# The first image's load in front of the weights, and side work between the first gathers, in a block-matching convolution kernel

## The chip, the cores and the metric

The kernel runs on one core of a Trainium2 chip. The metric is the device time of one execution in microseconds (us); smaller is better. A core has five engines with queues of their own: TensorE (PE, with its weight loads as PEld), VectorE (DVE), ScalarE (ACT), GpSimd (POOL) and SyncE (SP). SP, ACT and POOL issue DMAs in this kernel.

## The reference

Eight images of 32 channels and 128x128 pixels go through two layers. The first one normalises by groups of two channels, finds for each pixel the eight best of 25 shifts (of up to two pixels each way) by the squared difference over 3x3 patches, gathers the eight shifted copies, and runs a small convolutional network on the 256 channels. The second normalises again and applies one 5x5 kernel. Both add their input.

```python
def _patch_match_stack(x):                       # x: [8, 32, 128, 128]
    for dy in range(-2, 3):
        for dx in range(-2, 3):
            sh = x at (clip(y + dy), clip(x + dx))
            d = ((x - sh) ** 2).sum(1, keepdims=True)
            costs.append(_conv(d, ones_3x3, pad=1))
    _, idx = top_k(-costs, 8)
    return the 8 shifted copies of each channel  # [8, 256, 128, 128]

xb = _patch_match_stack(_gn(x))
dct = _conv(xb, dct_w, groups=C)
h = relu(_conv(_conv(xb, w1), w2, groups=CK, pad=1))      # w1, w3, w5: 256x256, 1x1
h = relu(_conv(_conv(h, w3), w4, groups=CK, pad=1))       # w2, w4, w6: depthwise 3x3
wiener = sigmoid(_conv(_conv(h, w5), w6, groups=CK, pad=1))
x = x + _conv(_conv(wiener * dct, inv_dct_w, groups=C), agg_w)
x = x + conv5x5(_gn(x), kernel)
```

## The kernel before

**Tiles.** An image lies in the tile xn: 128 partitions are 4 groups of rows times 32 channels, and each partition holds 38 rows (32 and a border of three) of 132 columns. load_image fills it with one large DMA for each row group (line 84, 32 partitions of 35 or 38 rows, 512 bytes a row) and six small ones that repeat the image's edge rows (line 89). The first image is loaded this way at the head of the program from ACT's queue, later ones from POOL's.

**Setup.** Behind the first image's DMAs in the text, SP loads the constants (cst), the depthwise weights (dwv, dwt) and the three 256x256 weights (nat_w1, nat_w3, nat_w5). POOL makes the block matrices dwd of the depthwise weights in 18 products (line 161); DVE reorders w1 (w_kc, line 178); TensorE transposes the three weights and ACT copies them to lw1, lw3 and lw5 (lines 188 and 189). The tiles of this setup have a pool of their own, with two PSUM buffers (ps_w).

**Matching.** For each image, prep takes statistics on DVE (st, line 348), normalises xn (line 359) and starts six rounds of squares: DVE subtracts shifted copies (df, line 413), ACT squares them (line 421), TensorE sums over channels (pd, line 428), ACT copies the sum to sm, and POOL stores it (sq). sources transposes the image to pixels first: TensorE (px), ACT (xs, line 384), POOL (DMAs xl, line 386, and xtd, line 394). costs loads the sums of one quarter of the rows of each row group into dsum (lines 461 and 468, 13 DMAs), sums them over 3x3 on DVE (v, line 477), transposes them (pt), copies them (ct, line 498) and picks the eight best with 32 pairs of maximum and index. places turns the indices to places (oc, then li, line 540) and stores them in DRAM (idxd).

**Gathering.** A unit is one step in gathering: gather_load fetches rows of pixels (xt) and the places, spread over the partitions (ib, line 574, from POOL); gather_select makes 0/1 selections from them on ACT (ib and sel, lines 588 and 589); gather_pixels multiplies them with the pixels on TensorE (pg, line 603) and ACT copies the result to xb (line 610). Buffers: five ib, four sel, three xt, four df, two ct.

**Order.** For PE, DVE and ACT the order of the program's text is kept (manual_schedule). All work that isn't the network itself is written as generators in four queues: D for work that costs DVE time, A for ACT, P and Q for TensorE. push puts a task in the queue that it names in a yield, with a cost and, as an optional third value, the number of turns before which it may not run. run("D", credit) takes tasks from D until their costs reach the credit; run of another letter takes all that are due. until repeats turns of D, A, P, Q until its condition holds. In the main loop, tick gives each step of the network its share of D. unit calls until by itself when gather_load needs places that aren't there yet. At the start prep(0) and mixes() (which makes ldct and lagg from dct_w, inv_w and agg_w) are pushed, and seven units are set off:

```python
for u in range(7):
    unit(gather_load, u)
    unit(gather_select, u - 2)
    unit(gather_pixels, u - 3)
```

Unit 0 needs the first quarter's places, unit 4 the second's. Everything behind this loop is the main loop, in which the three pointwise and depthwise convolutions of eight rows at a time, the gathers of the next rows and the side work of the next image are interleaved.

Of the kernel before, what the change touches and what calls it, by code (L numbers as in the profile page):

```python
# [8 lines left out]
F32 = mybir.dt.float32  # L9
# [6 lines left out]
P = 128  # L16
C, K, H, W = 32, 8, 128, 128
CK = C * K
NO = 25
R = 8  # L20
# [22 lines left out]
def bm3d_conv_preact(  # L43
# [16 lines left out]
    nc = tc.nc  # L60
# [9 lines left out]
    ps_x = ctx.enter_context(  # L70
        tc.tile_pool(name="ps_x", bufs=5, space=bass.MemoryType.PSUM)
    )
# [1 line left out]
        tc.tile_pool(name="ps_d", bufs=1, space=bass.MemoryType.PSUM)  # L74
    )

    def load_image(b, engine):

        xn = xnp.tile([P, HR, HX], F32, name=f"xn_{b}", tag="xn")
        for rg in range(4):  # L80
            s = slice(C * rg, C * (rg + 1))
            lo = 32 * rg - 3
            a, z = max(lo, 0), min(lo + HR, H)
            engine.dma_start(xn[s, a - lo : z - lo, 2 : 2 + W], x[b, :, a:z, :])
            for r in range(HR):
                y = lo + r
                if y < 0 or y >= H:
                    y = min(max(y, 0), H - 1)
                    engine.dma_start(
                        xn[s, r : r + 1, 2 : 2 + W], x[b, :, y : y + 1, :]  # L90
                    )
        return xn

    first = load_image(0, nc.scalar)
    cst = const.tile([P, C_N], F32, name="cst")
    nc.sync.dma_start(cst, consts)
    ident = cst[:, C_ID : C_ID + P]

    lw1 = const.tile([P, 2, CK], F32, name="lw1")
    lw3 = const.tile([P, 2, CK], F32, name="lw3")  # L100
    lw5 = const.tile([P, 2, CK], F32, name="lw5")
# [42 lines left out]
    nc.vector.tensor_scalar(inner, inner, -1.0, 1.0, op0=ALU.mult, op1=ALU.add)  # L144


    with tc.tile_pool(name="setup", bufs=1) as sp, tc.tile_pool(
        name="setup_ps", bufs=2, space=bass.MemoryType.PSUM
    ) as spp:
        dwt = sp.tile([P, 3, 4, 9], F32, name="dwt")  # L150
        for n, w in enumerate((w2, w4, w6)):
            for g in range(4):
                nc.sync.dma_start(
                    dwt[C * g : C * (g + 1), n],
                    w[:P].rearrange("(q c) o a b -> c q (o a b)", c=C),
                )
            nc.gpsimd.memset(dwd[0:C, n, 1], 0.0)
            for u in range(2):
                for dy in range(3):
                    s = slice(C * (u + dy), C * (u + dy + 1))  # L160
                    nc.gpsimd.tensor_tensor(
                        dwd[s, n, u],
                        cst[s, C_M32 : C_M32 + C]
                        .unsqueeze(1)
                        .unsqueeze(1)
                        .to_broadcast([C, 4, 3, C]),
                        dwt[s, n, :, 3 * dy : 3 * dy + 3].unsqueeze(3).to_broadcast([C, 4, 3, C]),
                        ALU.mult,
                    )
        wide = {}  # L170
        for name, w in (("w1", w1), ("w3", w3), ("w5", w5)):
            t = sp.tile([P, 2, CK], F32, name=f"nat_{name}", tag=f"nat_{name}")
            nc.sync.dma_start(t, w.rearrange("(m p) i a b -> p m (i a b)", p=P))
            if name == "w1":

                nat, t = t, sp.tile([P, 2, CK], F32, name="w1_kc")
                for m in range(2):
                    nc.vector.tensor_copy(
                        t[:, m].rearrange("p (k c) -> p k c", c=C),
                        nat[:, m].rearrange("p (c k) -> p k c", k=K),  # L180
                    )
            wide[name] = t
        for name, dst in (("w1", lw1), ("w3", lw3), ("w5", lw5)):
            for g in range(2):
                ps = spp.tile([P, CK], F32, name=f"ps_{name}_{g}", tag="ps")
                for m in range(2):
                    src = wide[name][:, m, g * P : (g + 1) * P]
                    nc.tensor.transpose(ps[:, m * P : (m + 1) * P], src, ident)
                nc.scalar.copy(dst[:, g], ps)

    xbp = ctx.enter_context(tc.tile_pool(name="xb", bufs=2))
    accp = ctx.enter_context(tc.tile_pool(name="acc", bufs=1))
# [21 lines left out]
    now = [0]  # L214

    def push(task):
        want = next(task, None)
        if want:
            which, cost, *wait = want
            queues[which].append((cost, task, now[0] + (wait[0] if wait else 0)))  # L220

    def run(which, credit=1e9):

        q, took = queues[which], 0.0
        for _ in range(len(q) if which != "D" else 1000):

            i = next(
                (
                    i
                    for i, (c, _, at) in enumerate(q)  # L230
                    if at <= now[0] and (c != PAIR or pairs[0] < 2)
                ),
                None,
            )
            if i is None or took >= credit:
                break
            cost, task, _ = q[i]
            del q[i]
            took += cost
            pairs[0] += cost == PAIR  # L240
            push(task)
        if which == "Q":
            pairs[0] = 0
        return took
# [8 lines left out]
    def group_stats(mv, name):  # L253
# [18 lines left out]
        yield from inverse_std(mr[:, 1:2], tmp[:, 0:1], tmp[:, 0:1])  # L272
        return mr

    def mixes():

        dq = work.tile([P, 2, K], F32, name="dq", tag="dq", bufs=1)
        src = dct_w.rearrange("(m h c i) k a b -> m h k c (i a b)", m=2, h=2, i=K)
        for k in range(K):
            for m in range(2):  # L280
                for h in range(2):
                    p = 64 * h + 8 * k
                    nc.sync.dma_start(dq[p : p + 8, m], src[m, (h + m + 1) % 2, k])
        m8 = work.tile([P, 8], F32, name="m8", tag="m16", bufs=1)
        yield "D", 1.0
        nc.vector.tensor_reduce(
            m8,
            cst[:, C_M32 : C_M32 + C].rearrange("p (a c) -> p c a", c=8),
            axis=mybir.AxisListType.X,
            op=ALU.add,  # L290
        )
        for m in range(2):
            nc.vector.tensor_tensor(
                ldct[:, m].rearrange("p (c i) -> p c i", i=K),
                m8.unsqueeze(2).to_broadcast([P, 8, K]),
                dq[:, m].unsqueeze(1).to_broadcast([P, 8, K]),
                ALU.mult,
            )

        iv = work.tile([P, 2, K], F32, name="iv", tag="iv", bufs=1)  # L300
        nc.sync.dma_start(iv, inv_w.rearrange("(m p) k a b -> p m (k a b)", p=P))
        ag = work.tile([C, CK], F32, name="ag", tag="xr")
        nc.sync.dma_start(ag, agg_w.rearrange("c i a b -> c (i a b)"))
        for m in range(2):
            yield "D", 0.5
            ib = work.tile([P, P], F32, name=f"ib_{m}", tag="xm")
            nc.vector.tensor_tensor(
                ib.rearrange("p (c k) -> p c k", k=K),
                cst[:, C_M16 : C_M16 + 16].unsqueeze(2).to_broadcast([P, 16, K]),
                iv[:, m].unsqueeze(1).to_broadcast([P, 16, K]),  # L310
                ALU.mult,
            )
            yield "P", 0
            ps = ps_x.tile([P, 512], F32, name=f"ps_ag_{m}", tag="x")[:, :C]
            nc.tensor.transpose(ps, ag[:, m * P : (m + 1) * P], ident[:C, :C])
            agt = work.tile([P, C], F32, name=f"agt_{m}", tag="agt")
            nc.scalar.copy(agt, ps)
            yield "P", 0
            ps2 = ps_x.tile([P, 512], F32, name=f"ps_ia_{m}", tag="x")[:, :C]
            nc.tensor.matmul(ps2, ib, agt, start=True, stop=True)  # L320
            nc.scalar.copy(lagg[:, m], ps2)
# [646 lines left out]
    def unit(stage, u, *rest):  # L968
        if 0 <= u < len(units) and units[u]:
            if stage is gather_load:  # L970
                at = (units[u][0], units[u][1] % 8 // 2)
                until(lambda: at in ready, 4.0)
            stage(*units[u], *rest)
# [13 lines left out]
    def tick(b, i):  # L987
# [3 lines left out]
        owed[0] -= run("D", owed[0]) if owed[0] > 0 else 0  # L991
        owed[0] = min(owed[0], 6.0)

    def until(cond, credit):
        while not cond():
            now[0] += 1
            run("D", credit)
            run("A")
            run("P")
            run("Q")  # L1000

    with tc.manual_schedule(engines=ORDERED):
        push(prep(0))
        push(mixes())
        xbd[0] = dram.tile([P, 2, H, W], F32, name="xbd_0", tag="xbd")
        for i in range(3):
            nc.gpsimd.memset(tb[i][0:64, :, 0], 0.0)
        for u in range(7):
            unit(gather_load, u)
            unit(gather_select, u - 2)  # L1010
            unit(gather_pixels, u - 3)
        u = 4
# [128 lines left out]
```

## Time and profile before

| what | value |
|---|---|
| median of 3 runs | 6841.84 us (6823.36 to 6853.25) |
| the profiled execution | 6843.88 us |
| its span, first to last instruction | 6842.1 us |
| mean granted TensorE clock | 0.976 |
| busy: PE, DVE, ACT, POOL | 93%, 86%, 74%, 47% of the span |
| DMA | 1021 MB, mean 149 GB/s |

The profile is of one execution. In its timeline a row has the start in us, the time from the first start to the last end of the merged instructions, engine and line, operation, tile written <- tile read, sizes and count, and in brackets how long the engine had stood and what ended that. A q behind an engine's name is its queue: there the row is the issuing of a DMA, not its transfer. A DMA that is named as the end of a wait is the one that came last by the profile, which can be another than the one waited for.

### The profile page before, as it was taken

Reading aid. Unit: us, or ns where it says so; the run is one execution under the profiler, and the core shown is the slowest. Engines: PE = TensorE matmul, PEld = TensorE weight load, DVE = VectorE, ACT = ScalarE, POOL = GpSimd, SP = SyncE. Lnnn points to the kernel's source line nnn. Section 1 sums busy time; section 2 is a strip of 40 time slices with the busy share of each in tenths; the row PEclk is TensorE's granted clock in tenths of the full one; section 3 lists DMA queues with packets and bytes.
Section 4 is the critical chain, followed back from the end, with each engine's and each line's share of the span. In section 5 each row is a group of like instructions: output and inputs, shape, how many; then the busy total and the mean of one; then the engine's idle time right before and its main releaser. Section 6 shows DMA issues by size and latency. Waiting matters only on the chain. (4 is left out here: it accounts for less than half of the span.)

```text
span 6842.1 us, 257025 instructions
## 1 busy us (share of the span) xinstructions
PE 6347.0 (93%) x113378; PEld 3356.7 (49%) x113378; DVE 5856.0 (86%) x8822; ACT 5064.5 (74%) x6698; POOL 3241.3 (47%) x5351
## 2 busy tenths in 40 slices
PE   4698999999999999999999999999999999999997
PEld 1354445455554445544554455555445455454553
DVE  6789988998889898898988898899888899877776
ACT  4687768777787777877778777877768777686772
POOL 6345436443464444644445444454435554344334
PEclk9899999999999999999999999999999999999998
DMA  3556656667566675665756667566665666566653
GB/s 80 135 148 151 155 138 162 154 161 155 144 158 160 148 167 137 162 148 154 163 134 158 164 147 168 136 165 158 151 148 148 159 160 149 138 168 156 155 151 77
DMA packets 809627, 1021.41 MB, mean 149 GB/s; under 512 B 255456, under 2 KB 619936, under 8 KB 808512
## 3 DMA queue, kind: packets, MB, share of 16 engines
q0 software_dynamic: 422432, 745.61, 43.8%
q1 hardware_dynamic: 381056, 256.86, 17.2%
q8 instruction: 892, 14.61, 0.9%
q10 hardware_dynamic: 5024, 2.49, 0.2%
q14 instruction: 223, 1.83, 0.1%
HBM read 553.25 MB, written 217.01 MB: 113 GB/s over the span
## 5 line engine op out<-in xcount | busy, mean ns | idle before, releaser
L695 DVE SCALAR_TENSOR_TENSOR acc<-tv,dwv,acc 128x1024 f32<-128x1024 f32 (+3 forms) x3264 | 4032.3, 1237 | 250.1 <-ACT acc L692 139.0
L721 PE MATMUL pw<-t,dwd 96*32 96x254 f32 (+7 forms) x31680 | 2143.5, 421 | 89.7 <-issue 41.9
L721 PEld LDWEIGHTS pw<-t,dwd 96*32 96x32 f32 (+1 forms) x31680 | 1107.0, 111 | 908.4 <-issue 437.1
L574 POOL DMA_DIRECT2D ib<-idxd x1024 | 570.8, 558 | 1780.0 <-ACT sel L589 1593.0
L588 ACT ACTIVATE ib<-ib,nplace 128x1024 bf16<-128x1024 bf16 x1024 | 1170.3, 1143 | 19.1 <-DMA ib<-idxd 19.1
L589 ACT ACTIVATE sel<-ib 128x1024 f32<-128x1024 bf16 x1024 | 1084.6, 1059 | 32.5
L665 PE MATMUL p<-acc,lw 128*32 128x256 f32 x16768 | 990.8, 382 | 23.8 <-ACT tv L649 22.7
L641 PE MATMUL pv<-acc,lw 128*128 128x512 f32 (+1 forms) x2112 | 973.5, 603 | 35.8 <-DVE acc L788 31.2
L761 POOL DMA_DIRECT2D xf<-xbd x1088 | 650.3, 631 | 321.2 <-PE pc L780 87.2
L665 PEld LDWEIGHTS p<-acc,lw 128*32 128x32 f32 x16768 | 556.2, 111 | 455.6 <-ACT tv L649 63.8
L649 ACT COPY tv<-pv 128x512 f32<-128x512 f32 (+2 forms) x784 | 437.9, 578 | 387.0 <-PE pv L641 378.3
L603 PEld LDWEIGHTS pg<-sel,xt 128*32 128x32 f32 x45056 | 576.2, 111 | 262.4 <-ACT sel L589 67.1
L421 ACT ACTIVATE df<-df 128x786 f32<-128x786 f32 (+2 forms) x576 | 467.9, 859 | 298.7 <-DVE df L413 295.9
L603 PE MATMUL pg<-sel,xt 128*32 128x48 f32 x45056 | 594.2, 207 | 90.4 <-ACT sel L589 47.5
L734 ACT ACTIVATE acc<-pw 128x512 f32<-128x512 f32 (+2 forms) x808 | 440.6, 573 | 256.4 <-PE pw L721 255.5
L413 DVE TENSOR_TENSOR df<-xn 128x786 f32<-128x786 f32 (+2 forms) x576 | 527.7, 967 | 118.7 <-PE pd L428 109.2
L641 PEld LDWEIGHTS pv<-acc,lw 128*128 128x128 f32 x2112 | 381.6, 191 | 477.6 <-issue 394.2
L699 ACT ACTIVATE acc<-acc 128x1024 f32<-128x1024 f32 (+3 forms) x408 | 417.0, 1022 | 229.7 <-DVE acc L695 229.5
L672 ACT COPY t<-p 128x512 f32<-128x512 f32 x800 | 424.6, 570 | 127.5 <-PE p L665 125.0
L692 ACT ACTIVATE acc<-tv,dwv 128x1024 f32<-128x1024 f32 (+3 forms) x408 | 454.6, 1114 | 50.6 <-PE pa L801 32.1
L641 PE MATMUL pv<-xb,lw 128*128 128x512 f32 x1024 | 476.2, 608 | 0.0
L665 PE MATMUL p<-xb,lw 128*32 128x256 f32 x8192 | 468.1, 380 | 3.5 <-DVE xy L906 3.5
(151 smaller groups left out, 5782.0 us busy)
## 6 DMA issues: line engine op xcount, KB each, us to landing
ib<-idxd POOLq DMA_DIRECT2D x1024, 256.0 KB, 4.5
xbd<-xb POOLq DMA_DIRECT2D x128, 1024.0 KB, 6.6
xf<-xbd POOLq DMA_DIRECT2D x960, 128.0 KB, 7.2
t<-t SPq DMA_DIRECT2D x792, 128.0 KB
t<-t SPq DMA_DIRECT2D x384, 256.0 KB
tv<-tv SPq DMA_DIRECT2D x384, 130.0 KB
xt<-xtd POOLq DMA_DIRECT2D x240, 176.0 KB, 4.6
xl<-xs POOLq DMA_DIRECT2D x256, 64.0 KB, 2.6
```

Of the source, the lines that this page charges most:

```text
L413: nc.vector.tensor_sub(df[:, :, ca:cz], xn[:, r0 : r0 + SR, ca:cz], xn[:, r0 + dy : r0 + dy + SR, ca + dx : cz + dx],)
L421: nc.scalar.activation(df[:, :, ca:cz], df[:, :, ca:cz], AF.Square)
L574: nc.gpsimd.dma_start(ib.rearrange("p k y x -> p (k y x)"), idxd[b][s4 // 8, s4 % 8, 4 * k0 : 4 * k0 + 8] .rearrange("k x -> (k x)") .part ...
L588: nc.scalar.activation(ib, ib, AF.Square, bias=nplace)
L589: nc.scalar.activation(sel, ib, AF.Relu, scale=-1.0, bias=1.0)
L603: nc.tensor.matmul(pg[C * j : C * (j + 1), :, xa:xz], xt[:, t], sels[j // 2][:, j % 2, :, xa:xz], start=True, stop=True,)
L641: nc.tensor.matmul(ps[:, :hr], lhsT[:, g, P:CK], src(g)[:, h : h + hr], start=g == 0, stop=g == 1,)
L665: nc.tensor.matmul(ps[C * r : C * (r + 1), e, :nb], lhsT[:, g, s], rows[:, r : r + 4 * nb - 3 : 4], start=g == 0, stop=g == 1,)
L692: nc.scalar.activation(acc, rows, AF.Copy, scale=tap)
L695: nc.vector.scalar_tensor_tensor(acc, rows, tap, acc, op0=ALU.mult, op1=ALU.add)
L721: nc.tensor.matmul(pt[u][C * j : C * (j + 1), ka:kz, :nb, xa:xz], dwd[0:hi, i - 1, u, j, dx + 1], t[0:hi, j, ka:kz, :nb, xa + dx : xz + dx ...
L761: nc.gpsimd.dma_start(xf[p : p + C, m, j0:j1], src[g, m, (h + m + 1) % 2, :, :, ya:yz])
```

## The change

Four edits. load_image takes several engines and gives them the row groups in turn: the first image is loaded from ACT (groups 0 and 2) and SP (groups 1 and 3), ahead of the constants and weights on SP. The setup of w1, w3 and w5 becomes a generator, weights, pushed between prep(0) and mixes(): its loads are issued there, its DVE work waits for at least eight turns, and the six pairs of transposes go one by one through the P queue; its tiles are parts of the main loop's acc tiles, and its PSUM comes from the common pool ps_x. The first DVE work of mixes may not run for ten turns. And in the loop over the first units, three turns of side work with a credit of 4.0 are run between the load of unit 2 and the selection of unit 0, and one between the load of unit 3 and the selection of unit 1.

```diff
-    def load_image(b, engine):
+    def load_image(b, *engines):
         xn = xnp.tile([P, HR, HX], F32, name=f"xn_{b}", tag="xn")
         for rg in range(4):
+            engine = engines[rg % len(engines)]
...
-    first = load_image(0, nc.scalar)
+    first = load_image(0, nc.scalar, nc.sync)
...
-        wide = {}
-        for name, w in (("w1", w1), ("w3", w3), ("w5", w5)):
-            t = sp.tile([P, 2, CK], F32, name=f"nat_{name}", tag=f"nat_{name}")
-            nc.sync.dma_start(t, w.rearrange("(m p) i a b -> p m (i a b)", p=P))
...
+    def weights():
+        natural, kc = {}, None
+        for i, (name, w) in enumerate((("w1", w1), ("w3", w3), ("w5", w5))):
+            t = accp.tile([P, 2, R * W // 2], F32, name=f"nat_{name}", tag=f"acc{i + 1}0")
+            natural[name] = t = t[:, :, :CK]
+            nc.sync.dma_start(t, w.rearrange("(m p) i a b -> p m (i a b)", p=P))
+        yield "D", 1.0, 8
+        nat = natural["w1"]
+        kc = accp.tile([P, 2, R * W // 2], F32, name="w1_kc", tag="acc31")
+        natural["w1"] = kc = kc[:, :, :CK]
+        for m in range(2):
+            nc.vector.tensor_copy(
+                kc[:, m].rearrange("p (k c) -> p k c", c=C),
+                nat[:, m].rearrange("p (c k) -> p k c", k=K),
+            )
+        for name, dst in (("w1", lw1), ("w3", lw3), ("w5", lw5)):
+            for g in range(2):
+                yield "P", 0
+                ps = ps_x.tile([P, 512], F32, name=f"ps_{name}_{g}", tag="x")
+                for m in range(2):
+                    nc.tensor.transpose(
+                        ps[:, m * P : (m + 1) * P],
+                        natural[name][:, m, g * P : (g + 1) * P],
+                        ident,
+                    )
+                nc.scalar.copy(dst[:, g], ps[:, :CK])
...
-        yield "D", 1.0
+        yield "D", 1.0, 10
...
+    def turn(credit):
+        now[0] += 1
+        run("D", credit)
+        run("A")
+        run("P")
+        run("Q")
+
     def until(cond, credit):
         while not cond():
-            now[0] += 1
-            run("D", credit)
-            run("A")
-            run("P")
-            run("Q")
+            turn(credit)
...
         push(prep(0))
+        push(weights())
         push(mixes())
...
         for u in range(7):
             unit(gather_load, u)
+            for _ in range({2: 3, 3: 1}.get(u, 0)):
+                turn(4.0)
             unit(gather_select, u - 2)
             unit(gather_pixels, u - 3)
```

In the two built programs the instructions of PE, DVE, ACT, POOL and SP differ in order only ahead of the second li copy; from there on they are the same, one by one. Ahead of it, w_kc comes behind the first 12 subtractions on DVE, the lw copies stand one by one between the squares of rounds 1 and 2 on ACT, dwd's 18 products stand directly ahead of the first xl DMA on POOL, the four xr_0 loads stand among the xl DMAs of POOL and the four xr_1 loads behind the first xt loads, and ACT runs unit 0's selections after six further squares of round 5, and unit 1's after the second ct copy.

More of the change, by code (lines that the diff above doesn't have):

```diff
@@ L144, in bm3d_conv_preact @@
     nc.vector.tensor_scalar(inner, inner, -1.0, 1.0, op0=ALU.mult, op1=ALU.add)
-    with tc.tile_pool(name="setup", bufs=1) as sp, tc.tile_pool(
-        name="setup_ps", bufs=2, space=bass.MemoryType.PSUM
-    ) as spp:
+    with tc.tile_pool(name="setup", bufs=1) as sp:
         dwt = sp.tile([P, 3, 4, 9], F32, name="dwt")
@@ L169, in bm3d_conv_preact @@
                     )
-        wide = {}
-        for name, w in (("w1", w1), ("w3", w3), ("w5", w5)):
-            t = sp.tile([P, 2, CK], F32, name=f"nat_{name}", tag=f"nat_{name}")
-            nc.sync.dma_start(t, w.rearrange("(m p) i a b -> p m (i a b)", p=P))
[L174 to L189, printed above, removed]
     xbp = ctx.enter_context(tc.tile_pool(name="xb", bufs=2))
```

## The prediction

> **What bounds the kernel now.** I read the page's forty slices first, then busy time by stretch, then the timeline of the start.
>
> ```profile
> span 6842.1 us, 257025 instructions
> ...
> PE   4698999999999999999999999999999999999997
> ...
> PEclk9899999999999999999999999999999999999998
> ```
>
> TensorE is full from the fifth slice on: only the first two slices, 342 us, have gaps that this change can touch.
>
> ```profile
> 0.00:20.00 20.00, 1.38 (x4) 0.69 (x4) 4.17 (x9) 0.00 (x0) 17.04 (x26) 1.00 0.64 118
> 20.00:40.00 20.00, 0.00 (x0) 0.00 (x0) 0.23 (x1) 0.94 (x1) 7.93 (x14) 1.00 0.41 66
> ...
> 140.00:160.00 20.00, 5.60 (x100) 3.06 (x100) 6.40 (x18) 11.25 (x13) 9.04 (x18) 0.56 0.46 136
> ...
> 300.00:320.00 20.00, 20.00 (x396) 11.16 (x392) 19.50 (x16) 17.70 (x24) 3.71 (x7) 1.00 0.51 124
> ...
> 2.00:4.00 2.00, 0.00 (x0) 0.00 (x0) 0.00 (x0) 0.00 (x0) 2.00 (x2) 1.00 0.94 249
> ...
> 22.00:24.00 2.00, 0.00 (x0) 0.00 (x0) 0.00 (x0) 0.00 (x0) 1.85 (x3) 1.00 1.18 226
> ...
> 32.00:34.00 2.00, 0.00 (x0) 0.00 (x0) 0.00 (x0) 0.00 (x0) 0.00 (x0) 1.00 0.95 215
> ```
>
> Columns are window, length, busy PE, weight load, DVE, ACT, POOL, then clock, DMA share, GB/s. For 40 us nothing computes, yet the DMA engines are half idle; when image data flows, it flows at 215 to 249 GB/s. From 300 us PE is full: what is saved ahead of that moves the end one for one.
>
> ```profile
> 0.74 0.43 ACTq L84 DMA_DIRECT2D xn<-in_x_dram  x1
> ...
> 8.14 16.09 POOL L161 TENSOR_TENSOR dwd<-cst,dwt 32x384 f32<-32x384 f32 x18 [1.66 <-DMA dwt<-in_L_conv_w_dram]
> ...
> 11.53 19.58 ACTq L84 DMA_DIRECT2D xn<-in_x_dram  x3
> ...
> 14.53 1.86 DVE L178 COPY w_kc<-nat_w 128x256 f32<-128x256 f32 x2 [7.80 <-DMA nat_w<-in_L_conv_w_dram]
> ...
> 37.29 1.74 ACTq L89 DMA_DIRECT2D xn<-in_x_dram  x3
> ...
> 41.02 4.84 DVE L348 BATCH_NORM_STATS2 st<-xn 128x6 f32<-128x512 f32 x8
> ...
> 45.90 0.37 DVE L352 BATCH_NORM_AGGREGATE mv<-st 128x2 f32<-128x48 f32 x1
> ...
> 50.14 2.89 DVE L359 TENSOR_SCALAR xn<-xn,mr_a 128x5016 f32<-128x5016 f32 x1
> ...
> 86.06 0.69 POOL L461 DMA_DIRECT2D dsum<-sq  x1
> ...
> 96.00 1.11 DVE L477 TENSOR_TENSOR v<-dsum 128x910 f32<-128x910 f32 x1 [4.89 <-DMA xl<-xs]
> ...
> 147.44 1.15 ACT L588 ACTIVATE ib<-ib,nplace 128x1024 bf16<-128x1024 bf16 x1 [9.40 <-DMA ib<-idxd]
> ...
> 156.43 0.50 ACT L498 COPY ct<-pt 128x400 f32<-128x400 f32 x1
> ...
> 182.19 0.48 ACT L540 CAST li<-pi 128x128 bf16<-128x128 f32 x2 [9.15 <-PE pi L538]
> ```
>
> The four large image loads are issued at 0.74, 11.53, 20.12 and 30.79, the last small one at 38.7. In the built program SP's and ACT's DMAs share eight semaphores in turn, and each waits for the DMA eight places before it; so the image waits on weight loads of SP, and they on it. Statistics start at 41.02, squares at 53.06. POOL issues DMAs without a gap over 0.2 us from 69.46 to 86.06, and DVE then waits 4.89 us for the dsum loads. At 138.03 ACT has written the first places and stands 9.40 us until they come back as ib; the squares' and costs' work behind it stands too.
>
> **What the Trainium skill says.** *DMA: Bandwidth & Descriptors*, "Issuing engines are not separate DMA queues": SP, ACT and GpSimd DMAs run on the same 16 engines and interleave, a second issuer saves issue time only. The trace agrees so far as 249 GB/s came from a single image load beside the constants; so I credit the second queue with no bandwidth, only with freed waits. *SBUF — State Buffer*, "Who interferes with whom": a GpSimd instruction that reads SBUF and a DVE instruction in a two-port mode, or with two SBUF inputs, take turns, the second fully blocked. The trace agrees for copies: at 14.53 two DVE copies took 0.97 us each amid POOL's dwd products, where a cast of the same 128x256 takes 0.28 (L520). For two-input subtractions beside dwd no run here shows it.
>
> **The change part by part.** T is when the image is in.
>
> 1. *Image.* Its ten DMAs now stand first; only SP's last two wait, for the first loads of either queue. 2.49 MB (queue q10) at 249 GB/s is 10.0 us; 0.74 issue, about 1.3 to first data (the window to 2.00 shows 12 GB/s), about 1.0 to land (data ended before 36, the next issue came at 37.29): **T = 13**. Bounds: 11.7 with no start-up to add; 24.3, if four loads cannot overlap and each takes the 5.9 us that 6.5 (30.79 to 37.29) less issue leaves.
> 2. *Statistics to squares.* Eight statistics 4.84, and some 0.5 for the five small constant operations now among them (an estimate; the last, L144, took 0.17); then 4.24 (45.90 to 50.14) and 2.89: squares at T + 12.6 = 25.6, without a lock.
> 3. *dwd.* The dwt loads now wait for the image's second ACT load (its semaphore). First products about 2 us after T, at 15 (iv, issued at 38.92, was used at 40.81). Alone 18 products end at 31.1, when the first xs copy is due (25.6 + 5.3), so they'd cost nothing. With the lock: four or five small DVE operations and the normalisation each meet a product of 0.83 half way, +1.9: squares at 27.5. By 24.6, 11 products are done, the normalisation blocks the next, 7 are left. They alternate with 7 subtractions of 0.90: 7 x 1.73 = 12.1, so dwd ends at 39.6 and the squares are 5.8 late.
> 4. *POOL to the first dsum load (86.06 now).* The third group of xl loads is issued when its xs copy is done, 13.4 behind the squares' start (66.49); from there POOL has no gap: five groups of xl (15.0), two of sq (4.5), and the four xr loads (2.5) that stood in idle time, 22.0. With the lock: 27.5 + 13.4 + 5.8 = 46.7 (POOL, free of dwd at 39.6 and of two groups at 45.6, isn't later), + 22.0 = 68.7: **17.4 gained**. Without: 25.6 + 13.4 + 22.0 = 61.0, **25.1**. ACT's moved copies (six lw at 0.4, four small ones) hide behind POOL: the seventh xs copy, 29.0 behind the squares now, comes at 27.5 + 29.0 + 5.8 + 1.4 = 63.7, and POOL turns to it at 65.7. DVE's moved pieces (about 2: two w_kc copies, ldct, ib) hide in its 4.89 wait, PE's transposes in its idle half; SP's 12 dwt, 3 nat and 32 dq loads, about 0.46 each unblocked, are issued by 35, the first needed after 38.
> 5. *From dsum to the places* nothing moves: the same order, DVE-bound (19.3 of 20 us).
> 6. *Turns.* The dsum sums of group 1 end at 141.8, transposes take 1.1: ct could be copied at 143.0 instead of 156.43, and the maxima start 13.4 earlier. ACT's eight ib and sel operations, 8.5 us, go between squares that leave it 1.7 idle each turn (1.67 to 1.69 in the timeline): the first four push the last squares and the second ct copy back, DVE waits some 2.8 for it against 1.3 now; the last four stand behind the second copy and run beside the maxima. POOL's new order puts the last dsum loads behind an ib load that waits for a selection; I put them out at about 170 on the old scale, when the indices are due. **11.9 gained** at the second li (182.19). Bounds 9.4, the stand alone, and 13.4.
> 7. *After that* every engine's instructions follow in the old order, and the gain is carried along; waits there are between them. The clock while PE starts is 0.50 to 0.64 and may change by little either way.
>
> Sum: 17.4 + 11.9 = 29.3. The profiled execution took 6843.88 (span 6842.1, 1.8 around it), 2.0 above the median 6841.84; 29.3 less is 6814.6 for such an execution, 6812.5 from the median.
>
> **Rivals.**
> - *A, as summed, lock and all:* 6812, own range 6800 to 6824. For it: the 0.97 us copies, the skill's sentence.
> - *B, no turn-taking between dwd and subtractions:* 25.1 + 11.9 = 37.0: 6805. For it: the trace has no such pair. Against: the copies.
> - *C, it doesn't do what it says: the loads stay serial behind one another.* T = 24.3, 11.3 worse than A: 18.0, 6824. For it: no two large image loads are ever in flight together in the trace. Against: at 13 to 18 us one shared the engines with the nat loads at 217 to 229 GB/s.
> - *D, slower: the granted clock.* From 300 us PE is the bound, some 6,500 us; each 0.01 of the mean clock (0.976 now) is worth 6,500 x 0.01 / 0.976 = 67 us. If 0.005 or more is lost, the gain is gone; with 0.0095 lost, 64 - 29 = 35 slower: 6876. For: the clock follows what ran before, and the start shows all from 0.50 to 1.00. Against: by 300 us it is at 1.00, and the work from there on is the same.
>
> **How the numbers follow.** 0.5%, about what a measurement of this kernel can tell from no change (its three runs span 0.44%), is 34 us. A has 0.55, B 0.33, C 0.05, D 0.07. A falls beyond 34 in four of ten (the working is good to some 5, a median to some 10), B in seven to eight of ten: faster 0.47. D gives slower over 0.5% in most cases: 0.06. The rest, 0.47, is within. The forecast is A's, 6812; the range, 6788 to 6832, takes in B with an early image, and C.
>
> **What would show it.** Right: statistics from 13 to 14, not 41; dwd products and first squares alternating, both near 1.7 us a pair; the first dsum load near 69; ACT with no wait over 3 us ahead of its first ib; second li near 153; then the old pattern, 29 earlier. dwd back to back and squares at 0.9 would mean B; image loads 6 us apart, C; a mean clock under 0.97, D. Wrong altogether: a new wait after the second li that gives the gain back.

## The result and the profile after

Over twelve executions each, the changed kernel takes 6803.94 us (median; 6798.84 to 6814.12) against 6833.18 for the kernel before: a ratio of 0.9959, 95% interval [0.9951, 0.9967], which is 28 us less (23 to 33). The profiled execution took 6809.07.

The page of the changed kernel, its span and two rows of its forty slices:

```profile
span 6807.3 us, 257036 instructions
...
PE   5798899999999999999999999999999999999997
...
PEclk8899999999999999999999999999999999999998
```

Only the first two slices have visibly more TensorE work than before. The clock row is not higher, and the mean granted clock of this execution is 0.973 against 0.976: the gain lies in the start, not in the clock. Busy time by stretch (window, length, busy PE, weight load, DVE, ACT, POOL, then clock, DMA share, GB/s):

```profile
2.00:4.00 2.00, 0.00 (x0) 0.00 (x0) 0.00 (x0) 0.00 (x0) 2.00 (x2) 1.00 0.98 210
...
12.00:14.00 2.00, 0.00 (x0) 0.00 (x0) 0.00 (x0) 0.00 (x0) 0.00 (x0) 1.00 1.28 180
...
16.00:18.00 2.00, 0.00 (x0) 0.00 (x0) 1.58 (x7) 1.27 (x1) 0.00 (x0) 1.00 0.24 20
```

The image flows without a break from 2 to 16 us at 180 to 210 GB/s, with the DMA engines' mean busy share above 1 from 4 us on (the times of several packets on one engine overlap). The 249 GB/s that the prediction counted on is not reached; what that number was stands below, under step 1. The timeline, queue by queue:

```profile
0.74 0.43 ACTq L85 DMA_DIRECT2D xn<-in_x_dram  x1
...
0.74 1.21 SPq L85 DMA_DIRECT2D xn<-in_x_dram  x2
...
23.42 22.99 SPq L291 DMA_DIRECT2D dq<-in_L_conv_dct_w_dram  x32
...
16.42 1.29 DVE L356 BATCH_NORM_STATS2 st<-xn 128x6 f32<-128x512 f32 x2 [15.49 <-DMA xn<-in_x_dram]
...
23.40 0.70 DVE L243 SCALAR_TENSOR_TENSOR tmp_a<-tmp_a,mv 128x1 f32<-128x1 f32 x1
...
26.77 3.31 DVE L367 TENSOR_SCALAR xn<-xn,mr_a 128x5016 f32<-128x5016 f32 x1
30.11 15.11 DVE L421 TENSOR_TENSOR df<-xn 128x792 f32<-128x792 f32 x12
...
18.10 21.87 POOL L160 TENSOR_TENSOR dwd<-cst,dwt 32x384 f32<-32x384 f32 x18 [10.14 <-DMA dwt<-in_L_conv_w_dram]
...
46.87 2.98 POOL L394 DMA_DIRECT2D xl<-xs  x4 [0.56 <-ACT xs L392]
...
68.67 0.69 POOL L469 DMA_DIRECT2D dsum<-sq  x1
...
120.48 0.41 ACT L548 CAST li<-pi 128x128 bf16<-128x128 f32 x2
...
125.84 0.49 ACT L506 COPY ct<-pt 128x400 f32<-128x400 f32 x1 [4.95 <-PE pt L502]
...
134.10 1.13 ACT L596 ACTIVATE ib<-ib,nplace 128x1024 bf16<-128x1024 bf16 x1
...
141.34 0.47 ACT L506 COPY ct<-pt 128x400 f32<-128x400 f32 x1
...
152.14 0.48 ACT L548 CAST li<-pi 128x128 bf16<-128x128 f32 x2 [3.87 <-PE pi L546]
...
163.91 0.56 POOL L567 DMA_DIRECT2D xt<-xtd  x1 [8.79 <-PE pg L611]
...
171.56 1.15 ACT L596 ACTIVATE ib<-ib,nplace 128x1024 bf16<-128x1024 bf16 x1 [9.47 <-DMA ib<-idxd]
```

Statistics start at 16.42 instead of 41.02, the first dsum load is issued at 68.67 instead of 86.06, and the second li cast starts at 152.14 instead of 182.19. ACT goes into its first ib at 134.10 without a wait for it; the squares and the ct copy of the next quarter now stand ahead of it. The wait of nearly 9.5 us that stands at 171.56 is an old one: the kernel before has it too, as 9.72 at 201.87.

### The profile page after: what moved, and what is told of

Same layout as the page of the kernel before. It is cut to its first block, busy times and chain, and to the rows that moved or that the text cites. A ratio compares the mean times of both kernels' runs of the same rounds, so it can differ in the third digit from the quotient of the medians.

```text
span 6807.3 us, 257036 instructions
## 1 busy us (share of the span) xinstructions
PE 6354.3 (93%) x113378; PEld 3352.8 (49%) x113378; DVE 5860.4 (86%) x8822; ACT 5064.6 (74%) x6698; POOL 3246.7 (48%) x5351
## 4 chain that ended last, share of the span: by engine, by line
PE 55%; DVE 23%; ACT 8%; DMA 6%; issue 5%; POOL 3%; SPq 0%; ACTq 0%; DVEq 0%; POOLq 0%
PE pw L729 18%; DVE acc L703 15%; PE pv L649 13%; PE p L673 12%; PE pg L611 4%; DVE df L421 3%; PE pc L788 2%; DMA t<-t 2%; PE p L902 2%; ACT df L429 2%; ACT ib L596 2%; DVE idx L514 1%; PE pa L809 1%; DMA xf<-xbd 1%; DVE acc L796 1%
```

## The experiments

Each ratio is to executions of the kernel before that were measured together with the run. From the ratio and their median I give microseconds: 0.001 is 6.8 us. Where a run is compared within its start, it is by the same instruction's start in the profile. Such starts scatter too, by up to 1.6 us: the first li of turns_only, ahead of which nothing was changed, starts 1.55 earlier than in the kernel before. Ends of single executions scatter by 10 us and more. "Lead" is how much earlier an instruction starts than in the profile of the kernel before, where the first four li casts start at 137.62, 182.19, 230.76 and 266.46.

**1. The two parts apart: the turns alone (turns_only), and all but the turns (no_turns).** The first is the kernel before with turn() and the loop; the second is the changed kernel without it:

```diff
-            for _ in range({2: 3, 3: 1}.get(u, 0)):
-                turn(4.0)
```

> The kernel before with the four turns of side work alone; image and weights load as before. Theory (the parts add up): statistics still start near 41, the first li stays at 138, ACT no longer stands for its first ib, the second li comes near 170 instead of 182.2, and all behind it follows: 12 us faster, ratio 0.998. Rival (the turns pay only behind the earlier image, or the saved wait comes back as another one behind the second li): second li near 170, but under 4 us at the end, ratio above 0.9994.

> The changed kernel without the four turns. Theory: the first dsum load stays at 68.7 and the first li at 120.5, ACT stands some 9.4 us for its first ib again, second li near 164.5: 17 to 18 us faster than before, ratio 0.9974. Rival (the turns carry the gain, the earlier image is lost in a wait for POOL): under 10 us, ratio above 0.9985.

Measured: turns_only 0.9992 [0.9984, 1.0], 5.5 us less; no_turns 0.9982 [0.9972, 0.9992], 12.3 less. The timeline of turns_only, then of no_turns, first and second li:

```profile
136.07 0.41 ACT L540 CAST li<-pi 128x128 bf16<-128x128 f32 x2
...
167.73 0.48 ACT L540 CAST li<-pi 128x128 bf16<-128x128 f32 x2 [3.87 <-PE pi L538]
```

```profile
120.71 0.41 ACT L548 CAST li<-pi 128x128 bf16<-128x128 f32 x2
...
130.53 1.15 ACT L596 ACTIVATE ib<-ib,nplace 128x1024 bf16<-128x1024 bf16 x1 [9.41 <-DMA ib<-idxd]
...
165.34 0.48 ACT L548 CAST li<-pi 128x128 bf16<-128x128 f32 x2 [9.20 <-PE pi L546]
```

What the turns remove is a wait of DVE for the ct copy behind ACT's first selections, here in the kernel before; in the changed kernel the same maximum starts at 126.36, right behind DVE's last subtraction.

```profile
156.96 0.20 DVE L505 MAX8 mx<-ct 128x8 f32<-128x25 f32 x1 [13.43 <-ACT ct L498]
```

From first to second li it is 31.66 us with the turns in either kernel (167.73 - 136.07; 152.14 - 120.48) and 44.63 and 44.57 without them: the turns are worth 12.9 to 13.0 us wherever the start stands. The rest of the change is worth the 16.9 by which the first li of no_turns leads. Together that is 29.8, against the changed kernel's 30.1. At the fourth li turns_only leads by 13.8 and no_turns by 16.4, together 30.2. At the end the two gains, 5.5 and 12.3, are smaller than the leads and than what was expected (0.998 and 0.9974). For the turns alone the whole interval, 0 to 11 us, lies below the lead of 13.8, so part of it was lost later on; where, these runs don't show. For no_turns the lead lies within the interval, 5 to 19 us.

**2. One queue for the image (one_queue).**

```diff
-    first = load_image(0, nc.scalar, nc.sync)
+    first = load_image(0, nc.sync)
```

> The changed kernel with the whole first image on SP's queue, still in front of all weights. Theory (being in front is what counts, the 16 DMA engines set the rate): image in at 15 to 18 us against 16.3, the first dsum load within 2 us of 68.7, the end within 2 us of the changed kernel, ratio 0.9955 to 0.9962. Rival (a queue alone makes no more than a large load in 6 us): image in at 24, everything 7 to 8 us later, ratio 0.997. Other rival (two queues disturb each other: 180 to 210 GB/s instead of 249): image in at 13, 3 us earlier, ratio 0.9955.

Measured: 0.9968 [0.9958, 0.9979]. Busy time while the image flows, then the timeline, DVE and ACT:

```profile
1.80:16.20 14.40, 0.00 (x0) 0.00 (x0) 0.00 (x0) 0.00 (x0) 6.16 (x13) 1.00 1.22 182
```

```profile
16.84 2.47 DVE L356 BATCH_NORM_STATS2 st<-xn 128x6 f32<-128x512 f32 x4 [15.91 <-DMA xn<-in_x_dram]
...
152.36 0.48 ACT L548 CAST li<-pi 128x128 bf16<-128x128 f32 x2 [4.12 <-PE pi L546]
```

Statistics start at 16.84, between the two profiles of the changed kernel (16.42, and 16.91 in after_again of experiment 5), and so does the second li (152.14, 152.36, 152.59). One queue keeps the transfers in flight just as well once nothing stands in front of them, so no gain of the second queue can be told from the scatter: what *DMA: Bandwidth & Descriptors* says in "Issuing engines are not separate DMA queues" holds here. Both rivals fall, the image at 24 and the image at 13. The ratio missed its range, 0.9955 to 0.9962, but its interval takes in the changed kernel's 0.9959.

**3. The load alone (load_only).** The kernel before with the image's load split over both queues, and the weights' work where it was:

```diff
-    first = load_image(0, nc.scalar)
+    first = load_image(0, nc.scalar, nc.sync)
```

> The kernel before with one part of the change alone: the first image goes over ACT's and SP's queues in turn; all weights, their transposes and the order of every engine's work stay as before. Theory (the place of the weights' side work on VectorE makes the front, not the load): the first statistics stand on VectorE behind the products that wait for SP's 32 dq loads; those are now issued behind two of the four image groups, as in the changed kernel, where they ended at 46.4 us against 38.9 in the kernel before. So the first statistics start at 48 to 49 us, not 40.2, the second li near 190 instead of 182.2, and the kernel is slower than before by about 8 us, ratio 1.001. Rival (the image's arrival is what was late): statistics at 16 to 25 us, a gain of 17 us as in the run without the turns, ratio 0.9975.

Measured: 1.0014 [1.0006, 1.0022], 9.6 us **slower**. (The kernel before starts its statistics at 41.02; the 40.2 of the expectation is the turns' run.) The timeline, SP's queue and DVE:

```profile
23.68 23.00 SPq L284 DMA_DIRECT2D dq<-in_L_conv_dct_w_dram  x32
...
46.64 0.23 DVE L294 TENSOR_TENSOR ldct<-m,dq 128x64 f32<-128x64 f32 x1 [20.26 <-DMA dq<-in_L_conv_dct_w_dram]
...
48.69 4.83 DVE L349 BATCH_NORM_STATS2 st<-xn 128x6 f32<-128x512 f32 x8
```

The image's last large load is issued at 3.12 on ACT's queue, as in the changed kernel, and the transfers run at 177 to 201 GB/s until 16 us; yet the statistics start 7.7 later than in the kernel before: on DVE, whose order is that of the text, they stand behind ldct and ib, products that need dq and iv, and SP is through with dq at 46.7. The lead at the first and second li is -7.6 and -7.5. So the early load is worth less than nothing here without moving the weights' side work behind the statistics.

**4. The lock: six products (six_products) and memsets in their place (memsets).** In the first, the second and third dwd groups are filled with zeros instead, so two thirds of the depthwise weights are left out:

```diff
+            if n:
+                nc.gpsimd.memset(dwd[:, n], 0.0)
+                continue
```

> The changed kernel with POOL's products for the first depthwise layer only: the twelve of the other two layers are left out and their blocks set to zero in POOL's idle time at the start. Lock theory: the six are done near 23.5, the normalisation takes 2.9 instead of 3.3, the first squares run at 0.9 us each instead of 1.5, the first dsum load comes near 64.5 instead of 68.7, and the end 4 us earlier than the changed kernel's, ratio 0.9953. Rival (POOL is late only because of its own DMAs, the lock costs nothing at the end): first squares at 0.9, but the first dsum load within 1 us of 68.7 and ratio 0.9959.

In the second, each product is replaced by two memsets:

```diff
-                    nc.gpsimd.tensor_tensor(
-                        dwd[s, n, u],
...
+                    for _ in range(2):
+                        nc.gpsimd.memset(dwt[s, n], 0.0)
```

> The changed kernel with its 18 GpSimd products for dwd replaced by 36 GpSimd memsets of 384 columns (two for each product) with the same waits; dwd is zero, so this part of the computation is left out. GpSimd is as busy beside VectorE's squares, but reads nothing. Theory (what alternates is the use of the port by any GpSimd instruction, as VectorE stood still in the kernel before while GpSimd wrote zeros at 4.5 us): squares that run beside memsets still take about 1.5 us each instead of 0.9, and end as late as GpSimd's work lasts. Rival (only GpSimd instructions that read lock VectorE out): every square takes 0.90 us as it does with six products, the normalisation 2.89, and the first dsum load is issued at 63.8 us or by GpSimd's own lateness, without long squares.

Measured: 0.9961 [0.9949, 0.9973] and 0.9956 [0.9942, 0.997]. First twelve subtractions and first dsum load of six_products; then POOL, the subtractions and the first dsum load of memsets:

```profile
29.21 10.77 DVE L424 TENSOR_TENSOR df<-xn 128x792 f32<-128x792 f32 x12
...
63.82 0.69 POOL L472 DMA_DIRECT2D dsum<-sq  x1
```

```profile
18.84 19.19 POOL L161 MEMSET dwt<- 32x384 f32 x36 [9.92 <-DMA dwt<-in_L_conv_w_dram]
...
29.80 7.23 DVE L414 TENSOR_TENSOR df<-xn 128x792 f32<-128x792 f32 x8
...
65.88 0.69 POOL L462 DMA_DIRECT2D dsum<-sq  x1
```

With POOL's products gone from that stretch, twelve subtractions take 10.77 us instead of 15.11 and the first dsum load comes 4.85 earlier. At the end nothing of this can be told: 0.9953 was expected of six_products, and its 0.9961 is nearer to the rival's 0.9959, with an interval that holds both. Beside memsets, which keep POOL busy until 38.0, the subtractions take 0.90 each (7.23 / 8), as if POOL stood still; that the first dsum load comes at 65.88 and not near 63.8 is POOL's own lateness, whose xl loads can start only at 37.97. My theory of this run fell: it is not any work of POOL's that locks out a two-input subtraction. What sets the products apart is that they read, as *SBUF — State Buffer* has it in "Who interferes with whom": with an instruction that reads, not with one that only writes. (A POOL instruction that reads one input only was not run.) The same page says that DVE in a two-port mode contends with GpSimd without that exception and that the one issued second is blocked. The longest of the products in the changed kernel and of the memsets here agree, if the normalisation runs in such a mode, which the trace doesn't name (minimum, median and maximum in ns):

```profile
L160 POOL TENSOR_TENSOR dwd<-cst,dwt x18: 827/832/3273, 18.1 to 38.5; 32x384 f32<-32x384 f32 x18
```

```profile
L161 POOL MEMSET dwt<- x36: 407/411/2927, 18.8 to 37.6; 32x384 f32 x36
```

One product and one memset are as long as the normalisation, 3.31 and 2.92 us, that they met. So a POOL that only writes is not always free beside VectorE. In the kernel before, a copy of 128x4 that takes 0.15 in the changed kernel took 2.04 beside POOL's memsets at the start, until the last of them ended at 6.5; that they held it up was not tested apart.

```profile
4.47 2.04 DVE L132 COPY neg<-cst 128x4 f32<-128x4 f32 x1 [3.54 <-DMA cst<-in_consts_dram]
```

**5. A version without the lock (later_products).** Nothing is left out: six products stay in place, twelve are issued once the main loop has begun, behind a copy on DVE (dwt in the constants' pool):

```diff
+    late = const.tile([P, C], F32, name="late")
...
+    products(0)
...
+                if s == 0:
+                    nc.vector.tensor_copy(late, cst[:, C_M32 : C_M32 + C])
+                    products(1)
+                    products(2)
```

> The changed kernel with only the six products of the first dwd group in place; the other twelve are issued on GpSimd once the main loop has begun, behind a copy on VectorE. Nothing is left out. Theory (twelve products beside the squares cost 5 us of the front, as the run with six products showed, and nothing waits for them until the first depthwise step): first dsum load at 63.8 us against 68.7, second li at 147.2 against 152.1; the order of GpSimd's loads around the third select step differs, so ACT's wait of 9.5 us for ib near 171 us may shrink too. End earlier than the changed kernel by 5 us, up to 14 if that wait goes: ratio to before 0.9955 to 0.9965 on this chip. Rival (the products lock out squares or selections later just as long, or a main-loop load waits behind them on GpSimd): no gain over the changed kernel in the same call, or a loss of up to 10 us.

> The changed kernel itself, on the same chip as the others of this call. If the second queue for the image is worth nothing, it stands where the run with one queue stood, within 3 us; if the lock's 5 us reach the end, the later products end 5 us ahead of it.

Measured side by side: later_products 0.9936 [0.9921, 0.9952], after_again (the changed kernel once more) 0.9961 [0.9949, 0.9974]; medians 6797.25 and 6816.16. The gain over the changed kernel is 17 us by the ratios, more than I expected, though the intervals overlap a little. (after_again stands 5 us below one_queue's ratio, not within 3; their intervals overlap widely.) The timeline of later_products:

```profile
64.05 0.69 POOL L476 DMA_DIRECT2D dsum<-sq  x1
...
147.50 0.48 ACT L555 CAST li<-pi 128x128 bf16<-128x128 f32 x2 [4.12 <-PE pi L553]
...
150.53 4.55 POOL L165 TENSOR_TENSOR dwd<-late,dwt 32x384 f32<-32x384 f32 x3
155.03 2.77 POOL L589 DMA_DIRECT2D ib<-idxd  x5
...
158.90 1.15 ACT L603 ACTIVATE ib<-ib,nplace 128x1024 bf16<-128x1024 bf16 x1 [1.44 <-DMA ib<-idxd]
...
187.77 0.48 ACT L555 CAST li<-pi 128x128 bf16<-128x128 f32 x2 [16.39 <-PE pi L553]
```

The second li leads by 34.7 (the lock's share, 4.6 over the changed kernel), the third by 43.0 against 30.3: another 8.1, as the wait for ib is 1.44 where it was 9.47. POOL's queue has another order here, with the xt_4 load behind the five ib loads; experiment 6 tests whether that is the reason.

**6. That wait by itself (xt_sync), and both (later_xt_sync).** In the changed kernel the xt_4 load waits on POOL's queue for TensorE until 163.91, and five ib loads stand behind it. In both runs SP issues it:

```diff
-                nc.gpsimd.dma_start(
+                (nc.sync if (b, s4) == (0, 4) else nc.gpsimd).dma_start(
```

> The changed kernel with one transfer moved to another queue: the xt_4 load, which waits on GpSimd's queue from 154.5 to 163.9 us for TensorE and has the ib loads of the second select step behind it, is issued by SyncE. Nothing is left out. Theory (this wait is what is late next once the first image is in early and the turns are taken): the five ib loads are issued at about 155.5 us instead of 165.35, ACT's wait of 9.5 us for ib at 171.56 us goes down to under 2, the third li cast comes near 191 instead of 200.4, and the end is 7 to 10 us earlier than the changed kernel's, ratio to before about 0.9948. Rival (ib's buffers, or TensorE's pixels, hold ACT up just as long): the wait keeps most of its 9.5 us or moves behind it, third li after 198, ratio 0.996.

> The kernel with the later products and the xt_4 load on SyncE's queue. In the run with the later products the wait for ib was 1.4 us already, so theory: no more than 1.5 us over that run, ratio to before 0.993 to 0.9945, third li at 186 to 188 us. Rival (the two gains add, 5 us of the lock and 9 of the wait on top of what the later products brought): third li near 180, ratio 0.992.

Measured: 0.9949 [0.9932, 0.9965] and 0.9943 [0.9929, 0.9957]. The timeline of xt_sync, SP's queue, POOL and ACT:

```profile
163.82 0.35 SPq L567 DMA_DIRECT2D xt<-xtd  x1
...
156.69 1.67 POOL L582 DMA_DIRECT2D ib<-idxd  x3 [0.52 <-DMA idxd<-li]
...
162.50 1.15 ACT L596 ACTIVATE ib<-ib,nplace 128x1024 bf16<-128x1024 bf16 x1 [0.22 <-DMA ib<-idxd]
...
191.39 0.48 ACT L548 CAST li<-pi 128x128 bf16<-128x128 f32 x2 [16.41 <-PE pi L546]
```

xt_4 is loaded no earlier, 163.82; but the ib loads no longer wait behind it, ACT's wait goes from 9.47 to 0.22, and the third li from 200.44 to 191.39: 9.1 us. With both, the third li comes at 188.67, near the 187.77 of the later products alone, so the wait that they had shortened is the one that this removes; the gains don't add. All three versions beat the kernel before, and their ratios lie 7 to 17 us below the two of the changed kernel (0.9959, 0.9961). Their intervals touch or overlap its; that they are faster than it rests on the leads of the start, and at the end is not shown for each. Which of the three is best these runs don't tell.

## Why the prediction was right, and where its sum was wrong

- **Case A came true**, 28 us against 29.3: products and subtractions alternate, the load's groups are in flight together (C would have had statistics at 24), the first dsum load at 68.67 for 68.7, the second li at 152.14 for 153. The median lies 8 below the forecast of 6812 because the kernel before has one of 6833.18 here, not 6841.84. Three of the signs missed: statistics at 16.42, not from 13 to 14; pairs of 1.53 us, not near 1.7; and a wait of ACT of 4.95 ahead of its first ib, where none over 3 was allowed. The last is for the transposes of ct, which need DVE's sums (they end at 124.6).
- **Step 1, T, was too small by 3.4:** 16.42 for 13. The failed term is the rate. The 249 GB/s of the kernel before from 2 to 4 us were not one load's. By DMA queue (packets, MB, share of the engines' time) that window holds 0.27 MB of the image from ACT's queue, q10, and 0.23 MB from SP's, q1, nearly all of it the constants:

```profile
q10 hardware_dynamic: 524, 0.27, 55.1%
q1 hardware_dynamic: 132, 0.23, 38.6%
```

  Nor is the best window of 2 us a load's rate. Over its whole stretch the last large load of the kernel before, with next to nothing beside it, has 160 GB/s; in the changed kernel the four together have 190 over theirs, some constants at the end included:

```profile
31.80:35.40 3.60, 0.00 (x0) 0.00 (x0) 0.00 (x0) 0.00 (x0) 0.00 (x0) 1.00 0.89 160
```

```profile
1.80:15.60 13.80, 0.00 (x0) 0.00 (x0) 0.00 (x0) 0.00 (x0) 6.16 (x13) 1.00 1.20 190
```

  The image's 2.49 MB took 13.8 us, about 180 GB/s, where the sum had 10.0; the parts around it were 0.4 shorter. My reason for giving the second queue no bandwidth was right (experiment 2).
- **Steps 2 and 3, the lock, were too dear.** Statistics to squares took 13.7 for 14.5. A pair of product and subtraction is no sum of 0.83 and 0.90: ACT's squares, which follow each subtraction of the changed kernel, start 1.53 to 1.54 apart:

```profile
31.65 0.86 ACT L429 ACTIVATE df<-df 128x792 f32<-128x792 f32 x1 [5.20 <-DVE df L421]
33.19 0.86 ACT L429 ACTIVATE df<-df 128x792 f32<-128x792 f32 x1 [0.67 <-DVE df L421]
```

  So the squares were 4.3 late (15.11 - 10.77), not 5.8. Case B's distance from A was overpriced too: 4.85 at the first dsum load, not 7.7.
- **Step 4.** From the squares' start to the third xl group I used the 13.4 of the kernel before; without the lock it is 12.4 (41.63 - 29.21 in six_products). So this point came out right because errors cancelled: +3.4 - 0.8 - 1.5 - 1.0 is +0.1, and the group was issued at 46.87 for 46.7. The 22.0 from there to the dsum load were 21.8. SP's dq loads took 0.72 each, not 0.46, and ended at 46.4, not 35; the 0.46 was wrong, but what needs them stands behind 20 subtractions, at 53.24, so it cost nothing. (In six_products, whose DVE is 5 us earlier, it waits 1.72 for them at 49.94.) In experiment 3, where they stand in front of the statistics, the same loads decide.
- **Step 6, the turns:** 12.9 for 11.9, close to the upper bound of 13.4: the second ct copy lost almost nothing to the selections.
- **Step 7** held as far as can be told: the fourth li leads by 30.1 as the second does. Further on single executions scatter: the spans of the two profiles of the changed kernel are 34.8 and 11.2 shorter than that of the kernel before, while the ratios give 28 and 27. A new wait that gives the gain back was not found. For the turns alone part of the lead was lost (experiment 1), so "one for one" isn't shown for each part.
- **D did not come.** The changed kernel's profile has 0.973, but that is one execution: over nine of the changed kernel (after_again) and 32 of the kernel before, measured together, the mean clock is 0.9757 and 0.9758. The price of D, 67 us for 0.01, was not tested and is not refuted: among those 32, the 15 with 0.974 or 0.975 have a median of 6844.6 us and the ten with 0.977 or 0.978 one of 6831.7, 13 us for a difference of some 0.0024. Whether the clock makes the time there, or waits of TensorE make both, isn't shown.

## What to carry to other kernels

Moving a load to the front pays only if the first consumer's engine has nothing else in front of it: look at that engine's order in the trace, not only at the transfer (experiment 3 lost 9.6 us with the load alone). Before a rate is taken from a window of a profile, see which queues' bytes are in it: the 249 GB/s were two transfers. Where an engine issues DMAs in order, one load that waits for a buffer holds back every load behind it; giving it another queue was worth the whole wait of 9 us at the third li. And before filling GpSimd's idle time beside a two-input VectorE stretch, see whether what it does reads SBUF: writing alone cost the subtractions nothing here.

## What was not expected of the hardware

- A large image load of 32 partitions by itself had a mean of 160 GB/s over its stretch, four together 190 from two queues and 182 from one. The DMA engines' mean busy share rose by a third with it, from 0.89 to 1.20 and 1.22, the rate by less than a fifth.
- A GpSimd product of 0.83 and a VectorE subtraction of 0.90 that take turns need 1.53 a pair: 0.2 less than if each kept the other out for all of its recorded time.
- A small two-input operation of VectorE (line 243, one column) took 0.70 beside the products, and 0.22 beside memsets: small ones pay for the lock too.
